# A twelve-stage perceiver on one core: preparation, second block and first router reordered, third round by batch, with a PSUM bank of the last attention lent to its second linear layer

## The chip, the cores and the metric

The kernel runs on one core of one Trainium2 chip, as one launch. The metric is the device time of one execution in microseconds (us); lower is better. PE is the matmul engine (TensorE), DVE VectorE, ACT ScalarE, POOL GpSimd, and SP the engine that issues most loads. A second number beside PE is its granted clock, 1.00 at full speed.

## What is computed

The state `x` has 2 batches of 128 tokens by 256 channels, all in float32. Four rounds follow one another, each with an attention over a context of 2048 tokens per batch, a token mixer and a feed-forward layer; each adds its result to `x`. Cut to what the change touches:

```python
# round 0: attention with 16 heads of 16 over the 4096 context tokens of both batches,
#          its operands rounded to integers; gated scan; 16 experts, 4 chosen per token
# round 1: x += softmax(x^ @ ctx.T / 16 + mask) @ ctx                 (x^: layernorm of x)
#          q, k = phi(x^ @ Wqk); v = x^ @ Wv
#          x += (q * scan(k*v) / max(sum_head(q * scan(k)), 1e-6)) @ Wout
#          x += soft mixture of 16 experts, over layernorm(layernorm(x)) * gamma + beta
# round 2: q = phi(x^ @ Wq); gate = sigmoid(x^ @ Wg + bg); kf = phi(ctx @ Wk)
#          x += (gate * (q @ (kf.T @ v)) / (q @ sum(kf) + 1e-6)) @ Wo
#          x += causal softmax attention, 16 heads of 16
#          x += x^ @ W + b + low-rank terms of the 2 best of 8 gates  (the linear layer)
# round 3: attention with 4 key heads of 128, 4 query heads each, over context and x;
#          a mixer with 64 heads; a gated feed-forward layer with packed weights
```

"The third round" below is round 2 of this list, "the second block" its round 1, "the last attention" that of round 3.

## The kernel before

The program is written with a tile library: engines and their order of priority are the program's, waits and queues are made from what each instruction reads and writes. An instruction may be put ahead of earlier ones of its engine when it is ready sooner. Where an engine is wrapped in `InOrder`, an instruction stays behind everything that was written before it on that engine. At run time each engine works its queue strictly in order. A tile with a tag and `bufs=n` has n buffers; a further tile of the tag waits for the release of the oldest.

**First attention (`l0_xattn`).** The preparation goes over ten steps `s`. In step `s` the unit of 512 keys `s` is projected on PE (`Keys.projected`), scaled with its row maximum (`scaled`, the DVE reduction 128x64), one step later rounded and split into bf16 parts (`quantised`, `first`), and two steps later completed (`second`, `third`), after which a DMA transpose on SP puts it into `kT`. The queries of batch `s` are made in steps 0 and 1. The values are projected in two halves of channels `c`, quarter by quarter: half 0 in steps 0 to 3, half 1 in steps 5 to 8 (`when`). Once the maximum of a half is known, `rounded` makes integers in `vw`, `turned_values` converts them into a tile `vb` with one buffer, and a DMA transpose moves them to `vi`; `spread` makes the scales of a half by a matmul of a diagonal `dg` with ones. All of these engines are in order.

The attention itself has 32 rounds, one for each head and batch. A round has four score matmul pairs, each copied out by DVE with its maximum (L539), an exponential over 4096 values on ACT to `Si` (L552, L555), a DMA transpose to `pT` (L556), and four rounds later 32 matmuls into `po` (L570). Rounds 0 and 1 are started first: six score passes, the conversions of the values' second half (L578), the last score passes and the exponentials. The last round is transposed on PE.

**First router (`l0_ffn`).** `ex`, a 0/1 matrix that spreads expert weights over channels, is made on POOL at the head of the layer (L669 to L676). The router runs batch by batch on small 128x16 tiles: softmax, the four best, mask, rank within the expert, weights split into three bf16 parts, transposed to `wT`. Then 25 chunks of weights stream through PE.

**Second block.** `l1_xattn` normalises both batches, computes the masked scores of both, then takes batch 0 and batch 1 through softmax, transposes and products. `l1_attn` runs once x of both is there, over two halves of channels `dc` for both batches. `l1_ffn` applies two normalisations and gamma and beta, normalises the rows (`xu`), transposes `xu` and `xl`, and streams the dispatch and combine products; the products with `W1` come after its first dispatch (L955 to L962).

**Third round.** `l2_xattn` makes the key features of 16 pairs of context tiles, eight per batch, each pair 3.6 us on PE, and three steps of unpacking the last layer's weights (`codes`) on DVE beside each. Then come its tail (state, normalisation, queries, gates, output), `l2_attn`, batch by batch with four head groups `j` each, and `l2_ffn`. `l3_xattn` is a generator: its first part, the 16 projections of the first group's keys and values with their rotation, does not need x and mixes with `l2_attn`; its second part opens its own PSUM pool `l3ps` (tags `wide`, `one`, `tr`, `py`, eight banks in all), normalises x, projects and rotates the query rows, turns the first group (L1339) and enters the loop over eight groups.

`g.psum()` is the pool of the middle part: four banks of tag `mm`, two of `tr`, two of `acc`. `g.load` takes weights into shared buffers of tags `w2` and `w4` (four each).

Of the kernel before, what the change touches and what calls it, by code (L numbers as in the profile page):

```python
# [22 lines left out]
P = 128  # L23
B = 2
# [291 lines left out]
def l0_xattn(g):  # L316
# [13 lines left out]
    with ExitStack() as ctx:  # L330
# [12 lines left out]
        def turned_values(c, n, pool):  # L343

            vb = pool.tile([P, 1024], BF16, tag="vb", name="vb", bufs=1)
            dve.tensor_scalar(vb, vws[n], UP, None, ALU.mult)
            nc.sync.dma_start_transpose(out=vi[:, 8 * n:8 * n + 8, c * P:(c + 1) * P], in_=vb)

        with tc.tile_pool(name="ctx0", bufs=1, reuse_waits="tile") as pc, tc.tile_pool(name="l0p", bufs=2, reuse_waits="tile") as p2, g.psum():
# [12 lines left out]
            bp = pc.tile([P, D], F32, name="bp")  # L362
# [14 lines left out]
            def queries(b, xnT):  # L377
# [57 lines left out]
            class Values:  # L435
# [27 lines left out]
                def spread(self):  # L463

                    dg = p2.tile([P, P], F32, tag="dg", name="dg", bufs=1)
                    dve.tensor_scalar(dg, g.ident, self.s, 2.0 ** 133 / UP, ALU.mult, ALU.mult)
                    ps = g.acc([P, P])
                    pe.matmul(ps, lhsT=g.ones, rhs=dg, start=True, stop=True)
                    act.copy(svb[:, self.c * P:(self.c + 1) * P], ps)
# [4 lines left out]
            xnT = g.transposed(g.layernorm())  # L474
            vals, units, late = [Values(0), Values(1)], [], None

            when = {n + 5 * c: (c, n) for c in range(2) for n in range(4)}
            for s in range(8 + 2):
# [21 lines left out]
                if s in when:  # L500
# [5 lines left out]
                    if c == 1:  # L506
                        turned_values(0, n, p2)
                if s == 5:
                    vals[0].spread()
                if s < 2:  # L510
                    queries(s, xnT)
            for n in range(4):
                vals[1].rounded(n)
            vals[1].spread()
            for b in range(B):
                dve.tensor_tensor(g.x[:, b, :], g.x[:, b, :], bp, ALU.add)

        with tc.tile_pool(name="l0s", bufs=2, reuse_waits="tile") as p2, tc.tile_pool(name="l0ps", bufs=1, space=PSUM, reuse_waits="tile") as pp:
# [59 lines left out]
            for n in range(4):  # L578
                turned_values(1, n, p2)
            for now in rounds:  # L580
                now.scores(3)
                now.weights(False)
            for n in range(2, len(todo) + LAG):
# [18 lines left out]
        with g.psum():  # L602
            g.out_project(g.transposed(o, "oT"), wp)

# [48 lines left out]
def l0_ffn(g, beside):  # L653
# [11 lines left out]
    with tc.tile_pool(name="l0f", bufs=2, reuse_waits="tile") as p:  # L665
        gw = p.tile([P, 2, E], F32, name="gw", bufs=1)
        nc.sync.dma_start(gw, g.ins["L0_ffn_gate_w"])

        ex = p.tile([3 * E, E * I], BF16, name="ex", bufs=1)  # L669
        nc.gpsimd.memset(ex[0:E, :], 1.0)  # L670
        nc.gpsimd.affine_select(out=ex[0:E, :], in_=ex[0:E, :], pattern=[[1, E * I]], compare_op=ALU.is_ge, fill=0.0,
                                base=0, channel_multiplier=-I)
        nc.gpsimd.affine_select(out=ex[0:E, :], in_=ex[0:E, :], pattern=[[-1, E * I]], compare_op=ALU.is_ge, fill=0.0,
                                base=I - 1, channel_multiplier=I)
        for k in range(1, 3):
            nc.gpsimd.dma_start(ex[E * k:E * (k + 1), :], ex[0:E, :])  # L676
# [17 lines left out]
        pls = []  # L694
        for b in range(B):
            pl = g.mm([P, E])
            g.project(pl, lambda c: xnT[:, c, b * P:(b + 1) * P], lambda c: gw[:, c, :])
            pls.append(pl)
        for c in range(2):
            projected(c)  # L700
        for b in range(B):
            pl = pls[b]
            nm = g.sm([P, 1], "nb")
            nc.vector.tensor_reduce(nm, pl, AX.X, ALU.max)
            nc.vector.tensor_scalar(nm, nm, -1.0, None, ALU.mult)
            s = g.sm([P, E], "s16")
            z = g.sm([P, 1], "z")
            nc.scalar.activation(s, pl, AF.Exp, bias=nm, accum_out=z)
            nc.vector.reciprocal(z, z)
            nc.vector.tensor_scalar(s, s, z, None, ALU.mult)  # L710
            t8 = g.sm([P, 8], "t8")
            nc.vector.max(t8, s)
            i8 = g.sm([P, 8], "i8", U32)
            nc.vector.max_index(i8, t8, s)
            f8 = g.sm([P, 8], "f8")
            nc.vector.tensor_copy(f8, i8)
            nc.vector.tensor_scalar(mask[:, b, :], g.iota16, f8[:, 0:1], None, ALU.is_equal)
            for k in range(1, 4):
                nc.vector.scalar_tensor_tensor(mask[:, b, :], g.iota16, f8[:, k:k + 1], mask[:, b, :], ALU.is_equal, ALU.add)
            ws = g.sm([P, 1], "ws")  # L720
            nc.vector.tensor_reduce(ws, t8[:, 0:4], AX.X, ALU.add)
            nc.vector.tensor_scalar(ws, ws, 1e-20, None, ALU.add)
            nc.vector.reciprocal(ws, ws)
            nc.vector.scalar_tensor_tensor(wgt[:, b, :], s, ws, mask[:, b, :], ALU.mult, ALU.mult)
        for b in range(B):

            rank = g.tr([P, E])
            nc.tensor.matmul(rank, lhsT=g.tri_lt, rhs=mask[:, b, :], start=True, stop=(b == 0))
            if b:
                nc.tensor.matmul(rank, lhsT=g.ones, rhs=mask[:, 0, :], start=False, stop=True)  # L730
            nc.vector.scalar_tensor_tensor(wgt[:, b, :], rank, 127.5, wgt[:, b, :], ALU.is_lt, ALU.mult)
            w3 = g.sm([P, 3, E], "w3", BF16)
            for k in range(3):
                nc.vector.tensor_copy(w3[:, k, :], wgt[:, b, :])
                if k < 2:
# [1361 lines left out]
```

## Time and profile before

| | us |
|---|---|
| median of 3 runs (1626.33 to 1632.14) | 1628.82 |
| the profiled execution | 1630.74 |
| its span | 1629.0 |
| preparation, until the first exponential starts | 116.83 |
| first attention, until its last transposed weights land | 288.4 |
| first router, from its first matmul to the first use of `wT` | 320.5 to 331.5 |
| second block, from x of round 0 to the first matmul of the mixture of experts | 411.7 to 493.4 |
| third round, from the first key feature to the first turned group of the last attention | 565 to 745.5 |
| loop over the eight groups, one group | 60.3 |

PE is busy for 1438.5 us of the span (88%), DVE for 1141.6, ACT for 817.8, POOL for 148.6. The chain of work that ended last is 61% PE and 12% DVE. A stretch of the table is read in the timeline from the first and the last instruction that its words name. The times of an instruction in the profile are its start and its duration; in square brackets stands how long its engine was idle before it and what ended that.

### The profile page before, as it was taken

The numbers are of one execution on the slowest core, as the hardware profiler recorded it, in microseconds if no ns is written. First come the engines' busy times: TensorE is split into PE (matmuls) and PEld (weight loads), VectorE is DVE, ScalarE is ACT, GpSimd is POOL, SyncE is SP. The second block draws the span as 40 slices with busy tenths as digits, with TensorE's granted clock in tenths as the row PEclk, the third lists the DMA queues.
The fourth block names the chain that finished last, engine by engine and source line by source line (L and its number), as shares of the span: only waits on it lengthen the run. The fifth ranks groups of instructions, "written<-read, shape, count | busy, mean of one in ns | idle before, by whom it ended". The sixth has DMA issues, their size and how long they took to land.

```text
span 1629.0 us, 17911 instructions
## 1 busy us (share of the span) xinstructions
PE 1438.5 (88%) x6686; PEld 903.5 (55%) x6686; DVE 1141.6 (70%) x1994; ACT 817.8 (50%) x1271; POOL 148.6 (9%) x140
## 2 busy tenths in 40 slices
PE   6749998699769997967999999999988899999978
PEld 4413333467445775744566666666544566666667
DVE  5759997477455476664756766766726899999976
ACT  2547776223222322323554554554545778888822
POOL 4720000202000000100000000000000111211110
PEclk9855555699879899958999999999999999999999
DMA  5769999744240131000000000000006122221100
GB/s 172 129 117 206 204 201 173 242 122 119 89 154 11 52 116 50 27 20 0 14 1 13 13 1 13 0 1 1 29 1 262 39 91 96 104 107 57 39 27 7
DMA packets 205614, 127.05 MB, mean 78 GB/s; under 512 B 177192, under 2 KB 184632, under 8 KB 202200
## 3 DMA queue, kind: packets, MB, share of 16 engines
q1 hardware_dynamic: 202720, 123.97, 30.1%
q10 hardware_dynamic: 2744, 1.76, 0.6%
q8 instruction: 53, 0.87, 0.2%
q14 instruction: 33, 0.27, 0.1%
q0 software_dynamic: 64, 0.18, 0.0%
HBM read 81.93 MB, written 0.26 MB: 50 GB/s over the span
## 4 chain that ended last, share of the span: by engine, by line
PE 61%; DVE 12%; ACT 7%; DMA 2%; issue 2%; SPq 0%; POOL 0%; DVEq 0%; ACTq 0%
PE wide L221 12%; PE mm L221 12%; PE mm L178 7%; PE py L221 7%; PE pb L221 5%; PE tr L221 4%; PE one L221 2%; PE acc L1045 1%; PE acc L221 1%; DVE bc L221 1%; DVE kq L221 1%; DVE ro L221 1%; PE pg L178 1%; ACT rot L1293 1%; PE acc L812 1%
## 5 line engine op out<-in xcount | busy, mean ns | idle before, releaser
L221 DVE TENSOR_SCALAR_CACHE_REDUCE S<-sc 128x1024 f32<-128x1024 f32 x128 | 150.4, 1219 | 4.6 <-ACT Si L221 2.4
L221 ACT ACTIVATE Si<-S,nb,sq 128x4096 int16<-128x4096 f32 (+1 forms) x35 | 122.7, 3506 | 52.8 <-issue 27.9
L221 PE MATMUL py<-pT,v 128*128 128x512 f32 x272 | 141.6, 606 | 5.0 <-ACT pT L1374 4.8
L221 PE MATMUL sc<-kT,qT 48*128 48x512 bf16 x256 | 131.0, 616 | 16.7 <-DVE S L221 15.5
L221 PE MATMUL wide<-kT,qT 128*128 128x512 f32 x256 | 121.4, 603 | 3.7 <-ACT v L1294 3.7
L1374 ACT COPY pT<-tr 128x512 f32<-128x512 f32 x136 | 78.4, 588 | 81.1 <-PE tr L221 81.1
L1363 ACT ACTIVATE S<-S,nb 128x2176 f32<-128x2176 f32 x32 | 67.5, 2108 | 95.0 <-DVE nb L221 95.0
L221 PE MATMUL pb<-wb,xT 128*128 128x512 f32 x256 | 112.7, 593 | 0.0
L221 DVE TENSOR_SCALAR_CACHE_REDUCE S<-wide 128x1024 f32<-128x1024 f32 x64 | 78.3, 1223 | 47.4 <-PE wide L221 47.0
L221 PEld LDWEIGHTS tr<-ident,S 128*128 128x128 f32 x544 | 68.0, 142 | 71.5 <-issue 42.5
L221 PE MATMUL wide<-w,ctxT 128*128 128x256 f32 x448 | 101.3, 379 | 0.0
L221 PEld LDWEIGHTS <-pT 128*128 128x128 bf16 x1024 | 36.4, 106 | 101.3 <-issue 86.2
L221 PEld LDWEIGHTS wide<-w,ctxT 128*128 128x128 f32 x448 | 83.0, 190 | 10.1
L221 PE MATMUL tr<-ident,S 128*128 128x128 f32 x544 | 81.4, 274 | 3.5 <-ACT S L1363 3.3
L221 PEld LDWEIGHTS pb<-wb,xT 128*128 128x128 f32 x256 | 48.8, 191 | 60.0 <-issue 55.9
L221 PEld LDWEIGHTS wide<-kT,qT 128*128 128x128 f32 x256 | 46.5, 192 | 58.3 <-issue 35.5
L221 DVE COPY kq<-wide 128x512 f32<-128x512 f32 (+1 forms) x44 | 27.2, 619 | 71.6 <-PE wide L221 67.6
L221 ACT ACT_TABLE_LOAD x53 | 68.0, 1283 | 4.0 <-PE mm L221 2.4
L221 ACT ACTIVATE bc<-pb,rs 128x128 f32<-128x128 f32 x256 | 68.2, 438 | 0.9 <-DVE rs L221 0.9
L221 ACT ACTIVATE bc<-pb 128x1024 f32<-128x1024 f32 x32 | 32.8, 1025 | 64.4 <-PE pb L221 64.4
L221 PE MATMUL mm<-m,xb 128*64 128x128 f32 x512 | 60.2, 275 | 2.9 <-DVE m L221 1.9
L221 PEld LDWEIGHTS mm<-m,xb 128*64 128x64 f32 x512 | 55.3, 137 | 6.7 <-DVE m L221 2.6
(503 smaller groups left out, 2913.2 us busy)
## 6 DMA issues: line engine op xcount, KB each, us to landing
w<-in_L_ffn_w_dram SPq DMA_DIRECT2D x25, 384.0 KB
ctxT<-in_ctxT_dram SPq DMA_DIRECT2D x16, 512.0 KB
wb<-in_L_attn_WB_dram SPq DMA_DIRECT2D x8, 1024.0 KB
wb<-in_L_attn_WC_dram SPq DMA_DIRECT2D x8, 1024.0 KB
bb<-in_L_attn_BC_bias_dram SPq DMA_DIRECT2D x8, 1024.0 KB
w<-in_ctx_dram SPq DMA_DIRECT2D x8, 512.0 KB
cx<-in_ctx_dram SPq DMA_DIRECT2D x8, 512.0 KB
wt<-in_L_attn_Wth_dram SPq DMA_DIRECT2D x8, 512.0 KB
```

The lines of the kernel that those rows point to most:

```text
L178: self.nc.tensor.matmul(out, lhsT=lhsT(c), rhs=w(c), start=(c == 0), stop=(c == n - 1))
L221: return lambda *a, **k: self.tc.keep_in_program_order(f(*a, **k))
L812: nc.tensor.matmul(av, lhsT=pT[:, i, :], rhs=cx[:, i, :], start=(t + i == 0), stop=(t + i == NT - 1))
L1045: nc.tensor.matmul(acc[c], lhsT=kf[:, i, c * P:(c + 1) * P], rhs=cx[:, t % 4 + i, :], start=(t + i == 0), stop=(t + i == NT - 1))
L1293: nc.scalar.activation(self.rot[:, t:t + n, :], kv[:, 0:n, 0, :], AF.Square)
L1363: nc.scalar.activation(Sf, Sf, AF.Exp, bias=nm, scale=SCALE, accum_out=self.rz[:, r:r + 1])
L1374: nc.scalar.copy(pT, tp)
```

## The change

**Preparation and first attention.** The transposes of the normalised x move behind the projections of step 0, the queries to steps 1 and 2. Half 1 of the values runs in steps 4 to 7. `turned_values` converts in place, in the bytes of `vw`. Both `spread`s and the addition of the bias `bp` move out of the preparation, behind the exponentials of rounds 0 and 1.

```diff
-        def turned_values(c, n, pool):
-            vb = pool.tile([P, 1024], BF16, tag="vb", name="vb", bufs=1)
+        def turned_values(c, n):
+            vb = vws[n].bitcast(BF16)
             dve.tensor_scalar(vb, vws[n], UP, None, ALU.mult)
...
-            xnT = g.transposed(g.layernorm())
-            when = {n + 5 * c: (c, n) for c in range(2) for n in range(4)}
+            when = {n + 4 * c: (c, n) for c in range(2) for n in range(4)}
...
-                if s == 5:
-                    vals[0].spread()
-                if s < 2:
-                    queries(s, xnT)
+                if s == 0:
+                    turned_queries()
+                if 1 <= s < 1 + B:
+                    queries(s - 1)
...
             for now in rounds:
                 now.scores(3)
                 now.weights(False)
+            for v in vals:
+                v.spread(p2.tile([P, P], F32, tag="dg", name="dg"), pp.tile([P, P], F32, tag="sv", name="sv", bufs=1))
             for n in range(2, len(todo) + LAG):
```

**First router.** `ex` is made by a function `gate_spread`, called ahead of `l0_attn`. The router works on 128x2x16 tiles, both batches in one instruction where the operation allows it; the four best and the masks stay per batch.

**Second block.** `l1_mixing` takes the place of `l1_xattn` and `l1_attn`. Its weights are loaded first. Both parts are generators per batch; the linear attention takes both halves of channels at once.

```diff
+        first, second = (context_attention(b) for b in range(B))
+        next(first)
+        next(second)
+        for _ in first:
+            pass
+        for _ in linear_attention(0):
+            next(second)
+        for _ in second:
+            pass
+        for _ in linear_attention(1):
+            pass
```

`context_attention(b)` yields after the scores and after each of four groups of context tiles, `linear_attention(b)` after normalisation, after phi, after the scans and at its end. In `l1_ffn` the two normalisations become one (scale 1 + 1e-5, eps 1e-10) with gamma and beta in two instructions, `xl` is transposed before `xu`, and the products with `W1` move ahead of the dispatch.

**Third round.** One function `l2` takes the place of three. All its weights and constants are loaded at its head, the constants into a pool at the right end of SBUF. Its parts are generators per batch; queries and gates are made first, the state's tail is reordered so that the denominator comes before the state.

```diff
+            first, second = (context_attention(px, b) for b in range(B))
+            next(first)
+            next(second)
+            for n, _ in enumerate(first):
+                if n >= NT // 2:
+                    next(second)
+            for _ in causal_attention(0):
+                next(second, None)
+            for _ in second:
+                pass
+        next(last)
+        third = linear(0, g.mm)
+        for _ in causal_attention(1):
+            next(third, None)
+            next(last)
+        next(last)
+        yield
+        for _ in linear(1, next(last)):
+            pass
```

`context_attention` yields after queries and gates, after each of eight pairs, after the copied state and after the masked state; `causal_attention` after normalisation, rotation, transposes, each of four head groups and its end; `linear` after normalisation, projections, router and its end. `linear` keeps its three products in one bank. For batch 0 it is a bank of tag `mm`; for batch 1 it is the bank `py`, which the last attention opens first and which its first group needs only later:

```diff
+        def normed(b):
+            g.norm_rows(xn[:, b, :], g.x[:, b, :])
...
+        now = Group(*todo[0])
         yield
-        now = Group(*todo[0])
         for t in range(0, NT, 2):
             now.projected(t, 2)
-        now.summed(0, NT)
+            if t == 8:
+                normed(0)
+                now.projected(NT)
+                now.summed(NT, NR)
+            if t == NT - 2:
+                now.summed(0, NT)
+            yield
+        now.rotated(NT, NR)
         now.rotated(0, 8)
         now.rotated(8, NT)
         yield
-        p2 = ctx.enter_context(tc.tile_pool(name="l3s", bufs=2, reuse_waits="tile"))
         g.ps = pp = ctx.enter_context(tc.tile_pool(name="l3ps", bufs=1, space=PSUM, reuse_waits="tile"))
         pe, dve = InOrder(tc, nc.tensor), InOrder(tc, nc.vector)
-        xnT = g.transposed(g.layernorm())
-        now.projected(NT)
-        now.summed(NT, NR)
-        now.rotated(NT, NR)
+        yield lambda: pp.tile([P, 512], F32, tag="py", name="py", bufs=1)
+        p2 = ctx.enter_context(tc.tile_pool(name="l3s", bufs=2, reuse_waits="tile"))
         for _ in now.turn():
             pass
+        normed(1)
```

The last attention's key/value pool `l3kv` also loses `reuse_waits="tile"`: its tiles now wait for every user of the pools whose bytes it takes, not only for those of the same bytes.

## The prediction

> **What bounds it now.** I read the stretches first (busy time by engine, granted clock), then the chain of waits, then the timeline in every stretch where TensorE (PE) is not full. The stretches that the edits touch; columns are the stretch and its length, busy us (count) of PE, weight loads, DVE, ACT and POOL, then granted clock, DMA share, GB/s:
>
> ```profile
> 120.00:275.00 155.00, 149.59 (x1162) 49.07 (x1161) 150.25 (x300) 118.22 (x63) 0.00 (x0) 0.50 1.14 202
> 458.00:494.00 36.00, 18.50 (x49) 12.94 (x49) 22.51 (x57) 9.46 (x19) 1.74 (x3) 0.64 0.37 123
> 565.00:628.00 63.00, 60.00 (x273) 49.77 (x272) 47.34 (x95) 14.09 (x22) 0.00 (x0) 1.00 0.28 84
> 628.00:646.00 18.00, 10.46 (x59) 7.86 (x57) 10.76 (x22) 7.87 (x10) 1.88 (x4) 1.00 0.24 67
> 646.00:708.00 62.00, 53.86 (x269) 42.66 (x270) 37.49 (x71) 22.39 (x58) 4.21 (x8) 0.78 0.08 26
> 708.00:730.00 22.00, 12.39 (x36) 8.23 (x34) 14.63 (x51) 4.49 (x11) 0.00 (x0) 0.55 0.05 13
> 730.00:746.00 16.00, 4.21 (x15) 2.40 (x16) 9.79 (x27) 1.88 (x6) 0.00 (x0) 0.86 0.05 16
> ```
>
> PE is full where it streams (565 to 628, and 778 to 1570, which no edit touches). The time to be won lies between streams: 17.5 us of idle PE in 458 to 494, 40 us in 565 to 746, and the preparation, where the timeline shows these waits:
>
> ```profile
> 12.40 1.40 PE L170 MATMUL tr<-ident,xn 128*128 128x128 f32 x4 [12.40 <-DVE rs L145]
> 13.59 5.72 PE L221 MATMUL mm<-wkv,ctxT 128*128 128x256 f32 x16
> 66.89 0.80 PE L221 MATMUL acc<-dg,ones 128*128 128x128 f32 x2 [10.06 <-DVE dg L221]
> 103.95 0.42 DVE L221 TENSOR_SCALAR vb<-vw 128x1024 bf16<-128x1024 int16 x1
> 107.56 0.43 DVE L221 TENSOR_SCALAR vb<-vw 128x1024 bf16<-128x1024 int16 x1 [3.19 <-DMA vi<-vb]
> 115.12 1.22 DVE L221 TENSOR_SCALAR_CACHE_REDUCE S<-sc 128x1024 f32<-128x1024 f32 x1
> 116.83 3.80 ACT L221 ACTIVATE Si<-S,nb,sq 128x4096 int16<-128x4096 f32 x1 [16.03 <-DVE nb L221]
> 125.89 3.80 ACT L221 ACTIVATE Si<-S,nb,sq 128x4096 int16<-128x4096 f32 x1 [1.39 <-DVE nb L221]
> 275.16 13.23 DMA pT<-Si
> ```
>
> The last line is from the chain of waits: the first attention ends on its DMA transposes. Each takes 5.2 us there (the last two land at 283.2 and 288.4), a round costs DVE and PE 5.1, and DMA is busy from 122 on. So 31 transposes in a row set the end: what counts is when the first one starts and whether the queue runs dry.
>
> **Preparation and first attention, from these rows.** Four terms.
> (1) Queries and their transposes move behind the first keys. Today the keys stand behind four transposes that wait for the layernorm until 12.40. By microsecond the loads move 1.7 MB up to 7 us; x, wkv and the first ctxT are 1.25 MB of it at even shares, so the keys can start near 9: 4 us (0 if wkv lands late, 5 if at once).
> (2) The scale of the values is no longer spread in the preparation. The PE queue stood 10 us for its diagonal; the reductions of key units follow every 7.5 us, only 62.03 to 74.32 takes 12.3: 4.8 us.
> (3) The values are turned in place, so the four conversions no longer wait for each other's DMA. From 103.95 to 115.12 remain four of 0.43 and two bias adds of 0.42. The value steps also end one step sooner, so the first six score passes start sooner; then the last key transpose binds (issued 94.85, DMA quiet at 102). The fourth score pass (PE 1.0, DVE 1.2, maximum 0.4) would bring the first exponential to 105 instead of 116.83: 11.8 us.
> (4) A new wait. Both spreads now stand between the second exponential and round 2, with one PSUM buffer: the second spread's matmul needs the first one's copy, which stands on ACT behind two exponentials of 3.8. Behind it in PE's program order wait the scores of round 2. With E the start of the first exponential: copy at E+7.9, scores at E+8.5, the third exponential at E+14.8, today E+9.06. Two transposes keep DMA busy to E+15, the third can start at E+19.2: DMA is dry for 4.1 us.
> Sum: 4+4.8+11.8-4.1 = 16.5, I take **16** earlier (8 if the start gives nothing and half of (3) is lost on a late key; 21 if the wait (4) is hidden).
>
> **Router of the first block.** The router for both batches in one pass drops some 14 of 46 small DVE instructions of 0.2 (2.8 us), but the rank matmuls still wait for PE's two chunks until 327: 1 us. The spread matrix (POOL 2.43+2.52+2.52 and two DMA issues) moves ahead of the second attention, past the gate memset of POOL at 305.15, which waits if the spread is late, and away from this row:
>
> ```profile
> 316.04 2.52 POOL L671 TENSOR_SCALAR_AFFINE_SELECT ex<-ex 16x2816 bf16<-16x2816 bf16 x1
> 316.21 2.50 DVE L156 TENSOR_SCALAR xn<-x,mv,rs 128x256 f32<-128x256 f32 x1
> ```
>
> The same normalisation costs 0.41 elsewhere: 2.1 us. Sum **3** (5 with all the instructions; 0 if the POOL work now falls on another normalisation). The Trainium skill ("SBUF — State Buffer", Who interferes with whom) has the pair of ports that DVE and GpSimd share as an exclusive lock; the row agrees. It speaks against the move as well: at 298.8 two normalisations would be hit instead, and by that the sum would be 1.
>
> **Second block.** PE gets batch 0's scores after one normalisation, without batch 1's, which waits today for the mask of batch 0 (first scores 419.65, then near 415): 4.5 us. Batch 0's linear attention runs inside batch 1's context attention, whose four steps leave PE only 3 us free in 436 to 458 (18.92 of 22); its PE work is some 6 us. So x of batch 1 comes at 457.9-4.5+6 = 459.4. These rows end the old tail:
>
> ```profile
> 457.94 0.48 DVE L813 SCALAR_TENSOR_TENSOR x<-acc,z,x 128x256 f32<-128x256 f32 x1 [3.81 <-PE acc L812]
> 491.36 1.23 PE L170 MATMUL tr<-ident,xu 128*128 128x128 f32 x4 [7.49 <-DVE xu L892]
> ```
>
> From x to PE's next stream (493.36) lie 35.4 us. New for batch 1: normalisation, transposes, copy 3.5 (457.94 to 461.46, unchanged), keys and queries 4, phi 2, scan, product and denominator matmul 3.3, maximum, reciprocal (1.75) and product 2.7, projection and residual 2.4: 17.9 against 26.0 (to 483.91), as the second half loop is gone. Then one normalisation with gamma folded in, one batch, transposes of xl first: 4.2, where 9.4 stand today, and the W1 matmuls, which are moved ahead, fill PE while xu is made. PE streams from 481.5 instead of 493.4: **12** (5 if the loads are late: w1's bytes come free only at the scan, and wqk, now ahead of the mask and ctx tiles on SP, holds one of their four buffers; 17 if the interleaved work falls wholly into gaps).
>
> **Third round.** Before: 181 us from 565 to the first transposed key group, with 141 us of PE. Its end:
>
> ```profile
> 745.52 5.15 PE L221 MATMUL tr<-ident,rot 128*128 128x128 f32 x21 [9.30 <-DVE rot L221]
> ```
>
> After: the same PE work, in which the first batch's tail and softmax attention lie beside the second batch's key features (8 x 3.6 us of PE), and the second batch's beside the first linear layer and the last attention's first projections. No cover is left for the second context tail (copies, transposes, two products, projection, some 8), for waits in the second softmax attention (its chain is about 33 us against 38 of PE around it; 4), and for the second linear layer in the lent bank. That one took 22 us (708 to 730) with 12.4 of PE; as 19 us of DVE rotations (four of 1.2, twelve of 0.7, the rest shorter) now fall beside it, I take 18 of wait. What followed it, 15.5 us from 730 to 745.5 (normalisation, projection and rotation of the query rows), is done for batch 0 while PE is busy. Every load of the round is now issued at its head, on the SP queue ahead of the ctx tiles; they are hidden while the key features stream.
> Sum: 137+8+4+18 = 167 of 181: **14** less. At full clock the work is 60+10.5+53.9x0.78+12.4x0.55+4.2x0.86 = 123, at today's 141; 137 is nearer today's, as much of it stays between waits. Bounds: 123, and 141 with 10 more of waits, so 28 and 0. The Trainium skill ("TensorE: Matmul & The Clock Gate", Part 1) has the full clock as long as PE has no idle window of 3.4 us. The first attention contradicts it: clock 0.50 with PE busy 97%. In the third round it would give rival E.
>
> **Sum.** The profiled execution ran 1630.74, its span 1629.0 and 1.7 around; the shown median is 1628.82, so it stands 0.1% above. 1630.7-16-3-12-14 = **1586**.
>
> **Rivals.**
> A, the transposes swallow the preparation: the DMA queue is the limit and (4) leaves it dry for longer, so only 5 of 16 remain: 1597. For: the chain ends on DMA. Against: the queue starts when its first input does.
> B, the third round keeps its length, its tail on DVE (rotations plus linear layer, 27 us) and its small matmuls limited by weight loads: 1600. For: DVE delays in 708 to 716. Against: 40 us of idle PE.
> C, slower: the in-order PE queue. Each of the eight softmax steps (two batches by four) has a chain of 6.4 us (0.69+0.69+1.28+1.1+0.69 and hops) beside 3.2 of its own PE work. If the fixed order puts key features behind the waiting transposes, 3.2 us are lost 8 times, and 2.4 (the wait of PE at 644.12 for the gated output) at each of some 25 other hand-overs of the batch-wise chains: 26+60 = 86 against 45 won, 1672; it decides from half of that. For: program order by batch. Against: today, with the same mixing at 646 to 708, PE idles 8 of 62.
> D, the reordering changes nothing, since the same instructions floated up already: 1629. Against: the waits of (2) and (3) are bound by buffers.
> E, the third round denser than I take it: no gap of PE is long, so it runs at 1.00 as from 565 to 628, with 123: 1572; with the other high bounds (21, 5, 17) 1560. For: the stretch before it. Against: 0.55 and 0.78 behind it.
>
> **How the numbers follow.** Forecast 0.50, A 0.15, B 0.13, C 0.10, D 0.02, E 0.10. Own range of the forecast 1570 to 1602. A measurement of this kernel tells 0.3%, about 5 us. Faster by more: forecast, A, B, E = 0.88; same 0.02; slower 0.10. The range holds A and B and the lesser part of E and leaves out C, D and its far end: 1563 to 1613.
>
> **What would show it.** Right: no gap between the four vb conversions; first exponential near 96 instead of 116.8, then a hole of 5 us before the third; last pT landing near 272; the normalisation ahead of the router at 0.41; PE's last stream in the second block 22 us after x of batch 1 instead of 35; turned keys some 45 us sooner than 745.5; the loop behind it unchanged at 60.3 us a group. Wrong: keys still at 13, PE idle above 15 us in the softmax steps, or a later stage longer than before.

## The result, and the profile after

The changed kernel takes 1608.22 us (median, 1602.62 to 1612.26) against 1629.28 before in the runs beside it: the ratio is **0.9868 [0.9832, 0.9905]**, 21 us faster, where 45 had been forecast. The profiled execution has a span of 1608.3 us (before 1629.0). Single executions of one kernel lie 4 to 22 us apart, so stages are judged below by several profiles.

Stages, in us, in the profiles of before and after:

| stage | before | after | change | forecast |
|---|---|---|---|---|
| start to the last transposed weights (preparation, first attention) | 288.4 | 268.2 | -20.2 | -16 |
| from there to the last matmul of the first block (holds the router) | 123.7 | 124.0 | +0.3 | -3 |
| from there to the last matmul of the second block | 155.0 | 150.8 | -4.2 | -12 |
| from there to the first turned group (third round) | 178.5 | 183.1 | +4.6 | -14 |
| from there to the end (not touched) | 883.5 | 882.2 | -1.3 | 0 |

The timeline of the changed kernel, first attention; a line is start, duration, engine and line, operation, output and input, and in brackets the idle time ahead of it and what ended it:

```profile
8.60 0.76 PE L221 MATMUL mm<-wkv,ctxT 128*128 128x256 f32 x1 [8.60 <-DMA wkv<-in_L_xattn_Wkv_dram]
91.02 1.43 DVE L221 TENSOR_SCALAR vw<-vw 128x1024 bf16<-128x1024 int16 x4
98.03 3.80 ACT L221 ACTIVATE Si<-S,nb,sq 128x4096 int16<-128x4096 f32 x1 [5.94 <-DVE nb L221]
99.82 0.79 PE L221 MATMUL sv<-dg,ones 128*128 128x128 f32 x2 [2.68 <-DVE dg L221]
105.91 0.80 PE L221 MATMUL sv<-dg,ones 128*128 128x128 f32 x2 [5.29 <-ACT svb L221]
112.94 3.80 ACT L221 ACTIVATE Si<-S,nb,sq 128x4096 int16<-128x4096 f32 x1 [5.93 <-DVE nb L221]
```

The keys start at 8.60 (13.59 before), the four conversions run without a gap, and the first exponential starts at 98.03. Then comes the forecast stall: the second spread's matmul waits 5.29 us for a copy on ACT, and the third exponential starts 14.9 us behind the first.

The second block's first scores, and the end of the third round, in the same timeline:

```profile
396.93 1.23 DVE L824 TENSOR_SCALAR bias<-m 128x2048 f32<-128x2048 uint8 x1 [1.99 <-DMA m<-in_mask_dram]
398.27 0.42 DVE L140 COPY xT<-tr 128x256 f32<-128x256 f32 x1
398.75 1.22 PE L178 MATMUL mm<-ctxT,xT 128*128 128x512 f32 x1 [3.32 <-DVE dd L806]
...
716.63 0.66 PE L1108 MATMUL tr<-ident,xn 128*128 128x128 f32 x2 [17.52 <-DVE xn L156]
```

The copy of the transposed rows stands on DVE behind the bias made from the late mask, and PE waits 3.32 us. (The profile names another small DVE write, which ended at the same moment as the copy.) At 716.63 PE has stood idle for 17.52 us, waiting for the normalisation ahead of the second linear layer. What DVE did in that time:

```profile
699.15 0.42 DVE L181 TENSOR_TENSOR x<-x,mm 128x256 f32<-128x256 f32 x1
699.49 2.28 DVE L1404 TENSOR_REDUCE rs<-rot 128x16 f32<-128x2048 f32 x1
702.95 1.22 DVE L1412 TENSOR_TENSOR kq<-kq,rs 128x1024 f32<-128x1024 f32 x1
...
711.89 0.42 DVE L151 BATCH_NORM_STATS2 st<-x 128x6 f32<-128x256 f32 x1
716.08 0.41 DVE L156 TENSOR_SCALAR xn<-x,mv,rs 128x256 f32<-128x256 f32 x1
```

x of batch 1 is complete at 699.57. Its statistics start 12.3 us later, as the sums and rotations of the last attention's keys stand ahead of them in DVE's queue. The third round by stretches of the same profile (length, then busy us and count of PE, weight loads, DVE, ACT and POOL, granted clock, DMA share, GB/s):

```profile
543.00:593.00 50.00, 45.47 (x228) 38.57 (x228) 37.72 (x80) 17.64 (x28) 1.65 (x4) 1.00 0.47 137
593.00:640.00 47.00, 41.99 (x177) 32.59 (x177) 27.57 (x50) 10.56 (x25) 2.77 (x3) 0.82 0.08 27
640.00:660.00 20.00, 16.79 (x76) 12.37 (x77) 10.30 (x28) 5.00 (x13) 0.13 (x1) 0.91 0.11 33
660.00:699.00 39.00, 35.76 (x162) 27.72 (x160) 22.82 (x59) 16.23 (x39) 1.76 (x2) 0.74 0.07 21
699.00:726.00 27.00, 7.04 (x20) 4.57 (x20) 20.64 (x47) 2.46 (x6) 0.00 (x0) 0.54 0.03 11
```

PE is busy for 147 of these 183 us. It idles for 16 us up to 699 and for 20 behind it. A first piece of the 16 is lost at the round's start, as the round now begins with the queries, which need the normalised x:

```profile
545.28 0.96 PE L1108 MATMUL tr<-ident,xn 128*128 128x128 f32 x4 [2.29 <-DVE xn L156]
```

Before, key features, which need no x, began at 565.07, 2 us ahead of the end of the second block's last matmul, and covered this wait. The two together are some 4 us that the new order gives away; no run tests them alone.

### The profile page after: what moved, and what is told of

Read it like the earlier page. It is cut to its first block, busy times and chain, and to the rows that moved or that the text cites. A ratio compares the mean times of both kernels' runs of the same rounds, so it can differ in the third digit from the quotient of the medians.

```text
span 1608.3 us, 17969 instructions
## 1 busy us (share of the span) xinstructions
PE 1444.2 (90%) x6732; PEld 908.3 (56%) x6732; DVE 1135.4 (71%) x1975; ACT 822.1 (51%) x1275; POOL 148.7 (9%) x140
## 4 chain that ended last, share of the span: by engine, by line
PE 73%; DVE 14%; ACT 7%; DMA 2%; issue 2%; POOL 1%; SPq 0%; ACTq 0%; DVEq 0%; POOLq 0%
PE mm L221 14%; PE wide L221 12%; PE mm L178 7%; PE py L221 7%; PE sc L221 6%; PE pb L221 6%; PE tr L221 4%; PE po L221 2%; PE acc L1147 2%; PE acc L221 2%; PE one L221 1%; DVE S L221 1%; DVE ro L221 1%; PE acc L1361 1%; DVE bc L221 1%
```

## The experiments

All ratios are to the kernel before, run beside each kernel on the same chip.

### Parts alone and parts undone

**The new third round alone.** The kernel before, with the functions `l2` and `l3_xattn` of the changed one.

> The kernel before with nothing but the new third round. Theory D (the new third round gives nothing back: 17.5 us of idle PE in front of its last normalisation and a lower granted clock eat the overlap; in the trace of the changed kernel it takes 183.1 us from the end of the second block's last matmul to the first turned group, against 178.5 before): 4 to 5 us slower than before, 1634. Theory P (the new third round does give the 14 us of the prediction, and what is missing was lost elsewhere): 1615. In the trace, by D, PE stands idle for some 17 us ahead of the transposes of the second linear layer's normalised rows.

Measured: 1624.65 us, 0.997 [0.9955, 0.9985], that is 5 us faster (2 to 7). Neither theory: the third round brings something, but a third of the forecast. The hole is there, in its timeline:

```profile
724.63 0.66 PE L1053 MATMUL tr<-ident,xn 128*128 128x128 f32 x2 [17.65 <-DVE xn L156]
```

The profiled execution was the fastest of eleven (1618.13), and its third round took 169.2 us, 14 less than the same code in the changed kernel's profile. The granted clock differs: the latter runs key features at half clock from 617 on (3.76 us for eight 128x256 matmuls, 1.97 in the other).

**The third round of before, in the changed kernel.**

> The changed kernel with the third round of before put back; preparation, router and second block stay changed. Theory D: 4 to 5 us faster than the changed kernel, 1603 to 1604, as the other parts brought 24 us up to the end of the second block. Theory P: 14 us slower than the changed kernel, 1622.

Measured: 1608.42 us, 0.9872 [0.9828, 0.9917]: the same as the changed kernel, within some 9 us either way. By the run above, the new third round is worth about 5 us, not 14; this run agrees within its noise.

**The new preparation alone.** The kernel before with the new `l0_xattn`.

> The kernel before with nothing but the new preparation and first attention. Theory (the prediction's first term, as the changed kernel's trace bears it out: last transposed weights at 268.2 instead of 288.4): 20 us faster, 1609 to 1610. Rival: half of it is given back in the first feed-forward layer, whose weights are then late: 1619.

Measured: 1614.45 us, 0.9908 [0.9889, 0.9927], 15 us faster (12 to 18). Its last weights land at 269.6, so up to there 19 of the 20 us are real. At the last matmul of the first block 16.3 are left: that stretch takes 126.2 here. Part of it is given back, less than the rival has it.

**The second block of before, in the changed kernel.**

```diff
-                l1_mixing(g, ctxT)
+                l1_xattn(g, ctxT)
+                l1_attn(g)
```

> The changed kernel with the second block of before put back (both batches normalised together, both linear attentions in one pass, two normalisations ahead of the mixture). Theory M (the dealt order costs most of what the rest of the block wins; landmarks of the changed kernel give the block 150.8 us from the first block's last matmul to the second's, 155.0 before): 3 to 5 us slower than the changed kernel, 1612. Theory P (12 us, as predicted): 1620. If the dealt order costs more than the block wins: 1600.

Measured: 1602.79 us, 0.9838 [0.9818, 0.9858], against 0.988 [0.9858, 0.9903] for the changed kernel in the same batch: not slower, rather some 7 us faster (2 to 12). The 12 us of the second block don't exist; its new order may even cost a little. The profiles don't show where these 7 us lie: the block takes 150.7 us here and 150.8 in both profiles of the changed kernel.

**The changed kernel again**, in that batch.

> The changed kernel once more, beside the others, for a second profile and a narrower interval: 1604 to 1612; the hole of 17 us ahead of the last normalised rows in the third round is there again, whatever the clock does; the stage lengths that differ by over 2 us from the first profile are those in which the granted clock differs.

Measured: 1609.66 us. Its second profile (span 1603.0) has the hole again, a third round of 181.4, and clocks of 1.00, 0.82, 0.91, 0.77 and 0.58 over nearly the same five pieces of it.

### The rotations ahead of the last normalisation

**Behind the linear layer.** The calls are written later, so that DVE may put the normalisation first.

```diff
-        now.rotated(NT, NR)
-        now.rotated(0, 8)
-        now.rotated(8, NT)
         yield
         g.ps = pp = ctx.enter_context(...)
-        pe, dve = InOrder(tc, nc.tensor), InOrder(tc, nc.vector)
         yield lambda: pp.tile([P, 512], F32, tag="py", name="py", bufs=1)
+        now.rotated(NT, NR)
+        now.rotated(0, 8)
+        now.rotated(8, NT)
+        pe, dve = InOrder(tc, nc.tensor), InOrder(tc, nc.vector)
```

> The changed kernel with the three rotations of the last attention's first group written behind the second linear layer, so that they only fill its gaps on DVE. Theory Q (order: the idle PE comes from 17 us of rotations that stand ahead of batch 1's normalisation in DVE's queue): the hole of 17.5 us ahead of the normalised rows' transposes shrinks to 7 or less, but as the 17 us of rotations must be done before the group is turned, the turn comes only 3 to 5 us sooner: 1604. Rival R (clock or PE's work sets the length, DVE waits anyway): hole smaller, turn at the same time, 1608. Rival Z (the wait is not on DVE's order): the hole stays 17 us.

Measured: 1600.74 us, 0.9815 [0.9789, 0.984]. In its timeline:

```profile
704.15 0.66 PE L1108 MATMUL tr<-ident,xn 128*128 128x128 f32 x2 [4.52 <-DVE xn L156]
714.14 0.37 PE L1289 MATMUL tr<-ident,gt 128*8 128x128 f32 x1 [4.04 <-DVE gt L1286]
717.88 2.73 PE L221 MATMUL tr<-ident,rot 128*128 128x128 f32 x12
```

The same instructions in another order: the hole falls from 17.5 to 4.5 us, a second one of 4.0 opens where the router's small steps wait for single rotations, and the turn comes 18.2 us behind the start of the last addition to x of batch 1 (26.9 in the changed kernel). That is 9 us, more than expected, since the turn starts on the first keys while the last are still rotated. The order of DVE's queue was the cause (theory Q).

**Half of the keys earlier**, in DVE's idle time during the second softmax attention:

```diff
             if t == 8:
                 normed(0)
                 now.projected(NT)
                 now.summed(NT, NR)
+                now.summed(0, 8)
+            if t == 10:
+                now.rotated(0, 8)
+            if t == 12:
+                now.rotated(NT, NR)
             if t == NT - 2:
-                now.summed(0, NT)
+                now.summed(8, NT)
             yield
-        now.rotated(NT, NR)
-        now.rotated(0, 8)
         now.rotated(8, NT)
```

> The changed kernel with the first half of the group's keys summed and rotated while the second softmax attention runs, where DVE is busy 59% of the time (22.8 of 39 us), and the query rows after it; the second half of the keys stays where it was. Theory Q: half of the 17 us goes into idle DVE time; the hole of PE falls from 17.5 to 8 or 9 us and the turn comes 8 to 10 us sooner: 1599. Rival R: softmax steps are delayed by as much as the hole shrinks, 1608.

Measured: 1595.54 us, 0.9791 [0.9766, 0.9815]; the hole is 7.02 us.

**Both edits.**

> The changed kernel with the first half of the keys rotated in the second softmax attention and the second half written behind the second linear layer. Theory Q: the normalised rows are transposed some 4 us after the residual instead of 7 (first half only) and 17 (changed kernel), the router's small steps wait for at most one rotation each, and the turn is 10 to 13 us sooner than in the changed kernel, 1 to 3 sooner than with the first half alone: 1594. Rival: the second half's rotations end after the linear layer and the turn waits for them, so it is no better than the first half alone, 1596.

Measured: 1596.65 us, 0.9807 [0.979, 0.9825]. The hole stays at 7.02: no better than the first half alone, the rival's number, but not for its reason. The turn waits for no rotation here; the hole did not shrink, since the first half's last rotations and the second half's first steps still stand ahead of the normalisation on DVE.

In the six profiles with one or both of these edits the third round takes 167.8 to 173.9 us (mean 170.1; the run with its dealing undone, below, is not counted). In the eight that have the new third round without them it takes 169.2 to 183.1 (mean 177.2), and in the three with the old one 178.4 to 179.3. The clock blurs these lengths. PE's idle time in the round is steadier: 40.1 to 41.4 us with the old round, 33.8 to 36.6 with the new one and 27.1 to 29.1 with the rotations moved (the run with matmuls that nobody reads is left out).

### The stall of the two spreads

```diff
-            for v in vals:
-                v.spread(p2.tile([P, P], ...), pp.tile([P, P], F32, tag="sv", name="sv", bufs=1))
+            sv = pp.tile([P, 2, P], F32, tag="sv", name="sv", bufs=1)
+            for v in vals:
+                v.spread(p2.tile([P, P], ...), sv[:, v.c, :])
+            act.copy(svb, sv.rearrange("p c j -> p (c j)"))
```

> The changed kernel with both scale spreads in one PSUM tile and one copy out, at the same place; so the second spread's matmul no longer waits for the first copy behind two exponentials. Theory W (the wait is what the prediction's step 4 says): the third exponential starts 9 us after the first instead of 14.9, and as the rounds, not the transposes, set the end (a round 5.0 to 5.1 us; last transposed weights 8 us behind the last exponential, in the kernel before 15 us), the last weights land 4 to 6 us sooner, 262 to 264 instead of 268.2: 1603. Rival A (the DMA queue of transposes sets the end): hole gone, landing within 1 us of 268: 1608.

Measured: 1599.14 us, 0.9811 [0.9783, 0.9839]. In its timeline:

```profile
98.72 3.80 ACT L221 ACTIVATE Si<-S,nb,sq 128x4096 int16<-128x4096 f32 x1 [5.89 <-DVE nb L221]
100.52 1.22 PE L221 MATMUL sv<-dg,ones 128*128 128x128 f32 x4 [2.69 <-DVE dg L221]
107.98 3.80 ACT L221 ACTIVATE Si<-S,nb,sq 128x4096 int16<-128x4096 f32 x1 [1.32 <-DVE nb L221]
```

The third exponential follows the first by 9.3 us instead of 14.9. The last weights land at 264.7; in the five profiles that have this edit, at 264.2 to 265.1 (mean 264.7), in ten with the new preparation and without it at 268.1 to 270.4 (269.0; the run with early masks is left out). The stall costs 4.3 us at the end of the attention; theory W holds. The median is 9 us below the changed kernel's; the two intervals leave 2 to 17, so what the edit brings beyond the 4.3, if anything, is not shown.

### The second block

**The two linear attentions side by side**, behind the context attention:

```diff
-        for _ in linear_attention(0):
-            next(second)
         for _ in second:
             pass
-        for _ in linear_attention(1):
+        for _ in zip(linear_attention(0), linear_attention(1)):
             pass
```

> The changed kernel with the linear attention of batch 0 no longer dealt between the steps of batch 1's context attention: both linear attentions are written behind it, step by step side by side. Theory M (the dealing cost what it won: from the first scores to x of batch 1 48.6 us in the changed kernel against 38.3 before): x of batch 1 comes some 39 to 42 us after the first scores, and the two linear attentions side by side need 3 to 6 us more than one; the block is within 3 us of the changed kernel's, 1605 to 1611. Rival N (dealing is worth a whole linear attention): 8 to 13 us slower, 1617 to 1621.

Measured: 1594.19 us, 0.9785 [0.977, 0.9801]: faster than either theory has it. Four stretches (from the first scores to x of batch 1, and from there to the first dispatch result), first of this kernel, then of the changed one:

```profile
395.00:434.00 39.00, 35.37 (x128) 22.60 (x129) 15.69 (x26) 8.11 (x10) 0.00 (x0) 0.93 0.29 86
434.00:479.00 45.00, 31.92 (x124) 20.36 (x123) 26.52 (x58) 9.52 (x18) 1.84 (x3) 0.85 0.26 90
```

```profile
399.00:447.00 48.00, 40.91 (x160) 27.51 (x160) 22.11 (x37) 11.31 (x13) 0.72 (x1) 0.91 0.26 77
447.00:489.00 42.00, 29.96 (x98) 18.19 (x97) 20.55 (x48) 8.89 (x17) 0.82 (x2) 0.80 0.26 88
```

Dealt between batch 1's steps, batch 0's linear attention adds 5.5 us of PE and 3.5 us of idle PE ahead of x of batch 1. Behind x it takes only 3 us away, 2 of PE and 1 of idle PE. That the second linear attention fits into the waits of the first there is a reading of these rows; no run shows it apart.

**Masks early, their bias on ACT.** Masks and decay are loaded on ACT's queue ahead of the first feed-forward layer.

```diff
-            nc.vector.tensor_scalar(bias, m32.bitcast(U8), 1.0, 1e30, ALU.subtract, ALU.mult)
+            nc.scalar.activation(bias, m32.bitcast(U8), AF.Identity, bias=low, scale=1e30)
```

> The changed kernel with masks and decay loaded ahead of the first feed-forward layer, and the mask's bias made on ACT instead of DVE. Theory V (the first scores of the second block wait for the copy of the transposed rows, which stands on DVE behind the bias of the late mask and the decay's copy): first scores 3 us after the transposes of the normalised rows begin falls to 1.5, that is 3 us sooner after the last matmul of the first block (6.6 to under 4): 1605. Rival: ACT's bias takes the place, no change, 1608.

Measured: 1608.95 us, 0.9865 [0.9843, 0.9887], no change. In place, theory V holds: the first scores come 3.8 us after the first block instead of 6.6. Yet the last weights of the first attention land at 275.0, not 268.2. The order of ACT's queue had shifted with the new loads, as its timeline and chain of waits show:

```profile
261.16 1.50 ACTq L242 DMA_DIRECT2D row<-in_L_ffn_b_dram  x1
261.99 12.97 DMA pT<-Si
```

This load, which gathers pieces of 4 bytes, is issued at 272.81 in the changed kernel, when the transposes are done. Here it meets the last of them, and that one takes 13 us instead of 7.

### Together, and what was still open

**Four edits together**: the spreads in one tile, both edits of the rotations, the linear attentions side by side.

> The changed kernel with four edits together: the two spreads in one PSUM tile, the first half of the keys rotated early, the second half written behind the second linear layer, the linear attentions side by side behind the context attention. If the gains lie in stages of their own and add (9, 12 and 13 us by the medians against the changed kernel's 1608): 1574. If part of them was the clock of the few runs: 1580 to 1586. Rival: they overlap, no better than the best of them, 1594.

Measured: 1579.28 us (1576.96 to 1584.37), **0.9692 [0.967, 0.9715]**, faster than both kernels. The medians do not add: some 29 of 34 us do. Whether the rest was the clock of the single runs or an overlap of the edits, no run separates.

**The same again.**

> The kernel with four edits once more, as the base of the others on the same chip: 1577 to 1584.

Measured: 1580.43 us, 0.9685 [0.9659, 0.9711].

**Less one, the linear attention dealt again.**

> The kernel with four edits, less one: the linear attention of batch 0 is dealt between the steps of batch 1's context attention again. Theory M (the dealing costs some 5.5 us in its own stage: from the first scores to the first dispatch result 84.4 us without it, 89.9 with it): 5 to 6 us slower than with four edits, 1585. If the 13 us by which the medians differ (1609 against 1594) are the dealing's: 1592. If they were luck of the clock: 1579 to 1581.

Measured: 1589.44 us, 0.9755 [0.9727, 0.9783], 9 us slower than beside it without dealing. The price is real. By the profiles of all runs:

| second block, us | old order (4) | dealt (10) | side by side (4) |
|---|---|---|---|
| last matmul of block 1 to first scores, mean | 7.8 | 6.6 | 6.5 |
| first scores to x of batch 1, mean | 37.5 | 48.5 | 38.9 |
| x of batch 1 to first dispatch result, mean | 52.8 | 41.4 | 45.6 |
| dispatch result to the block's last matmul | 54.3 to 55.3 | 51.2 to 65.1 | 51.2 to 54.3 |

(In the first line the run with early masks is left out.) Up to the dispatch result the dealing costs 5.4 us. Against the run beside it, this run's own profile loses another 3 in the last line, which none of the edits touches. There the length goes with the granted clock: 51.2 us at 1.00, 54.3 at 0.94, and 63.7 and 65.1 at 0.79 and 0.76, where the mixture of experts runs at half clock for some 25 us (three of the ten dealt profiles).

**The third round's dealing undone**, on the kernel with four edits:

```diff
-            for n, _ in enumerate(first):
-                if n >= NT // 2:
-                    next(second)
-            for _ in causal_attention(0):
-                next(second, None)
+            for _ in first:
+                pass
             for _ in second:
                 pass
+            for _ in causal_attention(0):
+                pass
```

> The kernel with four edits, and the third round's context attentions written one after the other ahead of both softmax attentions, instead of batch 1's key features being dealt between batch 0's softmax steps. Theory O (there the dealing is worth its while: batch 1's key features, 8 x 3.6 us of PE, are what covers batch 0's softmax chain): 10 to 25 us slower, 1590 to 1605. Rival (dealing costs in the third round as in the second block): 3 to 8 us faster, 1573.

Measured: 1588.8 us, 0.9738 [0.9713, 0.9764], 8 us slower; its third round takes 176.4 us against 169.6. There the dealing pays (theory O's direction, though below its 10 us). Its reason, that the dealt matmuls cover waits, isn't borne out. The round in the kernel with four edits, repeated, and then in this one:

```profile
529.60:699.20 169.60, 141.89 (x661) 112.50 (x661) 117.55 (x262) 54.42 (x111) 6.31 (x10) 0.87 0.20 58
528.40:704.80 176.40, 147.83 (x661) 117.35 (x662) 119.54 (x262) 57.29 (x113) 6.50 (x10) 0.82 0.18 56
```

PE idles for 27.7 us with the dealing and 28.6 without it. What differs is the time of the same matmuls, at a clock of 0.87 against 0.82. Batch 1's key features depend on nothing in batch 0's softmax chain, so dealing them adds no waits; why the clock is lower without it stays open.

**Matmuls that nobody reads, in the hole** of the changed kernel's third round.

```diff
+        still = one()
+        for k in range(24):
+            nc.tensor.matmul(still, lhsT=g.ident, rhs=ctxT[:, k % 2, 0:512], start=True, stop=True)
         yield lambda: pp.tile([P, 512], F32, tag="py", name="py", bufs=1)
```

> The changed kernel with 24 matmuls that nobody reads (128x512, some 10 us at full clock) in the hole ahead of the second linear layer's normalised rows. Theory K (PE's granted clock falls because PE stands idle): the hole stays, but the linear layer behind it runs at 0.9 or more instead of 0.54, and the turn comes 9.4 us after the transposes of the normalised rows in the changed kernel, 6.5 to 7.5 here: 1606. Rival (the clock in this stretch is a budget that other work has used up): 9.4 us as before, 1609.

Measured: 1612.2 us, 0.9863 [0.9829, 0.9897]. These matmuls took 20.8 us, not 10 (the trace has 48 of them for the 24 written), and delayed the normalised rows' transposes by 3 us, so the total tells nothing. The stretches do; first the hole and the linear layer behind it in the changed kernel, then the same in this one:

```profile
699.00:716.60 17.60, 0.12 (x1) 0.00 (x0) 17.43 (x32) 0.70 (x3) 0.00 (x0) 0.55 0.05 15
716.60:726.10 9.50, 7.02 (x20) 4.59 (x21) 3.20 (x16) 1.75 (x3) 0.00 (x0) 0.50 0.01 2
```

```profile
703.00:723.60 20.60, 20.60 (x50) 9.13 (x49) 17.91 (x33) 0.83 (x3) 0.00 (x0) 1.00 0.04 13
723.60:731.10 7.50, 4.12 (x21) 2.67 (x20) 2.85 (x15) 1.75 (x3) 0.00 (x0) 1.00 0.00 0
```

With PE kept busy, the clock is 1.00 instead of 0.50 and the linear layer takes 7.3 us instead of 9.4 (theory K, in the one profile). So that hole costs 2 us beyond its length.

## Why the prediction was right in parts and wrong in sum

**Preparation and first attention, 16 forecast: right, in part by luck.** 15 us by the run with it alone. Its working held: keys at 8.60 (near 9), no gap between the conversions, first exponential at 98.0 (96), the third 14.9 us behind it (14.8). The last weights landed even earlier than 272, at 268.2. A load of 4-byte pieces (the bias row of the mixture), issued at 274.42 in the kernel before, had met its last transpose, which took 13.23 us; now it is issued at 272.81, behind the last transpose, which takes 7.04. That part, some 6 us, was not forecast: the forecast's own steps come to 18.8 less 4.3, that is 14.5. That the stall of step (4) costs 4.1 is borne out by 4.3. The rival in which the transposes swallow the preparation falls with it.

**First router, 3 forecast: borne out for the normalisation, on average for the rest**, not in the one profile. The normalisation takes 0.41 again, in every profile with the new router:

```profile
296.26 0.41 DVE L156 TENSOR_SCALAR xn<-x,mv,rs 128x256 f32<-128x256 f32 x1
```

The matrix is now made from 259 to 267, beside copies on DVE that keep their 2.49 us (2.48 before), and hits no normalisation. The stretch from the last weights to the block's last matmul is 121.6 us in the mean of 14 profiles with the new router (118.5 to 124.9) and 124.9 in the three with the old one (123.7 to 126.2). The granted clock of that stretch differs as well, and no run has the router alone.

**Second block, 12 forecast: wrong; the first of the failed steps.** The step that failed is "So x of batch 1 comes at 457.9-4.5+6". The 4.5 was 1.2, because the mask that had held up batch 1's normalisation now holds up the copy of batch 0's transposed rows, which is behind its bias in the same DVE queue. And the 6 of interleaved PE work was 11.0 (48.5 against 37.5): the PE work comes with waits of its own in an in-order queue. What followed was sized well: 11.4 us saved behind x of batch 1, 13.4 forecast. The sum up to the dispatch result is 1.6 us by these means and nothing between the changed kernel (96.5 from the first block's last matmul) and the one with this block undone (96.4); the lower clock of the mixture in some executions comes on top.

**Third round, 14 forecast: wrong; the second.** The run with it alone gives 5. "137" for PE and "8", "4" and "18" of waits made 167. Two terms were mis-sized. The waits: 30 in the sum, 34 to 37 in the seven profiles counted above (40 to 41 with the old round), so the new order takes 5 us of idle PE away and not 10. In the changed kernel they are 16 and 20; the wait for x at the round's start was not in the sum. The PE time: 137 in the sum, 135 to 147 in these profiles (138 with the old round), 147 in the changed kernel's, where the clock is 0.54 to 0.91 behind the first 50 us. Its sign of being wrong, a later stage longer than before, came in that profile. The 18 for the second linear layer was a fair price. What failed in reasoning is that it was priced as a slowed linear layer, with the rotations "beside" it: they stood ahead of it, in a queue that works in order, and they can be moved. With them moved the third round takes 170.1 in the mean instead of 177.2. The 137 was not impossible, since one profile came to 169.2 with the hole still in it; but it needs a clock that most executions don't get.

**The rivals.** B, the third round keeping its length, comes nearest: it named a tail of 27 us on DVE, and the trace has 26.9. Its 1600 still held the 12 us of the second block. C, the loss through the in-order PE queue, has its mechanism in that block's dealing, at a small part of its price. E, full clock in the third round, did not come about.

## What to carry to other kernels

When work of one batch is dealt between the steps of another, ask of each dealt piece whether its inputs have long been there. Key features from the context pay (8 us here); a linear attention that hangs on the batch just finished brings its own waits into the in-order queue and costs (5 us in its own stages, 9 by the medians). Look, for the normalisation or copy that everything waits for, at what is ahead of it in its own engine's queue: 17 us of work that was merely written earlier were worth 7 to 13 us. And where the granted clock is well below 1, a forecast from sums of PE time needs two values, not one.

## What the runs showed of the hardware

The clock was the surprise. In the mixture of experts the same instructions ran at 1.00 in some executions and at half in others, as these stretches show, of the kernel with early masks and then of the one with both linear attentions side by side:

```profile
500.00:520.00 20.00, 17.88 (x110) 13.90 (x108) 13.79 (x29) 9.59 (x15) 0.00 (x0) 1.00 0.09 27
520.00:545.00 25.00, 24.81 (x98) 18.13 (x98) 3.88 (x12) 3.31 (x10) 0.00 (x0) 0.51 0.00 1
```

```profile
500.00:520.00 20.00, 17.69 (x127) 13.65 (x126) 10.24 (x23) 8.46 (x15) 0.00 (x0) 1.00 0.08 27
520.00:531.00 11.00, 10.13 (x74) 7.35 (x70) 2.94 (x9) 3.23 (x6) 0.31 (x4) 1.00 0.37 73
```

Ahead of both lies a stretch in which PE is busy for 88 to 89% with no wait over 1.3 us. In one the clock then fell to 0.51 for 25 us, with PE 99% busy; in the other it stayed. What decides it is open. The Trainium skill ("TensorE: Matmul & The Clock Gate", Part 1) explains the clock by activity in a free-running window of about 3.4 us, so that its changes vary from run to run. The hole that was filled with matmuls agrees (1.00 instead of 0.50); the 25 us at half clock with PE busy, as the profile counts it, do not.

The load of 4-byte pieces beside the last DMA transpose goes with a transpose of 12.97 us instead of 7.04, of 13.23 in the kernel before, and of 11.48 in that kernel with the new third round; in all three the load is issued 0.7 to 0.8 us ahead of the transpose. In the fifteen other profiles the load is issued behind the landing, and the last transpose takes 6.78 to 7.04. No run moves the load by itself.
